# Eight PSUM banks divided anew, and row gathers asked for in fives, in a two-layer relational graph network on one core

## The chip, the cores and the metric

The kernel runs on one core of a Trainium2 chip. A core has a matrix engine (TensorE, PE in the profile, with its weight loads as PEld), VectorE (DVE), ScalarE (ACT), GpSimd (POOL) and SyncE (SP), which issues transfers. They run side by side, each in its own order, and wait for one another through semaphores. TensorE writes its results into PSUM, which has eight banks of 128 partitions by 512 numbers of 32 bits. VectorE and ScalarE read them from there.

The metric is the time of one execution on the device, in microseconds (us). Lower is better.

## The reference

50,000 nodes with 128 features each and 850,000 edges with a relation out of 16. The edges are sorted by destination, and each node has an edge to itself. Two layers of a relational graph convolution are followed by a residual sum and a layer norm:

```
def _rgcn_layer(h, src, dst, rel, basis, w_comp, loop_w, bias):
    W = jnp.einsum('rb,bio->rio', w_comp, basis)
    seg = dst.astype(jnp.int32) * N_REL + rel.astype(jnp.int32)
    agg = jax.ops.segment_sum(h[src], seg, num_segments=N_ENT * N_REL)
    agg = agg.reshape(N_ENT, N_REL, -1)
    msg = jnp.einsum('nri,rio->no', agg, W)
    out = msg + h @ loop_w + bias
    return jax.nn.relu(out)

h = _rgcn_layer(x, src, dst, rel, basis1, w_comp1, loop_w1, bias1)
h = _rgcn_layer(h, src, dst, rel, basis2, w_comp2, loop_w2, bias2)
x = _layernorm(x + h, axis=-1)
```

There are 8 bases. In words: for each edge the row of its source node is fetched, weighted by 8 numbers that belong to its relation, summed by destination, multiplied by the 8 bases and added up.

## The kernel before

**Tiles and chunks.** The edges other than those of a node to itself stand in tiles of 128. Ten tiles are a chunk (`K = 10`), and a layer has 625 chunks (`C`), 6,250 tiles in all. Since the edges are sorted by destination, a tile touches few nodes. It has 12 slots (`WN`), and a chunk has 120 (`S`).

**Gathers.** For each tile GpSimd issues one indirect transfer (`gather`, line 178) that fetches 128 rows of 128 numbers from `x` in layer one and from `H1` in layer two (`g<-in_x_dram,src` and `g<-H,src` in the profile). The rows land in one of 30 tiles `g0` to `g29` (`RING * PER`, 6 by 5). A tile `g` is free again when the product with it has run. At the start of a layer 30 gathers are issued at once (line 956). After that, `fetch` (lines 939 to 943) is called at line 996 after each chunk's last product, for the ten tiles that lie three chunks ahead. Of the ten gathers the first waits for TensorE, and this one wait covers all ten. `row_of` (line 934) says which of the 30 tiles a gather takes: on every second turn through the ring the order within ten is reversed, so that the first gather of a ten takes the tile whose product ran last.

**Products.** For each tile TensorE multiplies the 128 rows with `hot` (line 982), 128 by 96: for each edge its slot and its 8 weights. A product takes two passes, which the profile counts as two matmuls. Five products fill a bank `pa` of the pool `ps_a`, and ScalarE copies it into `aT` (line 999). `hot` is made by VectorE at line 872 two chunks ahead, from the weights of lines 596 and 625 (`weights`, every second chunk).

**Work beside the products.** TensorE's order is written out by hand: `ordered` at line 859 keeps the order in which the program names the instructions. After each of a chunk's ten products `beside` (line 911) takes one step of generators. With t as the tile's place in the chunk, these are:

- `owning` at t = 4 and 9: steps of `from_itself` (line 661), which handles groups of 512 nodes. Four transposes go into a bank `po` (line 676, two, a `yield`, two more). ScalarE copies them out (line 680). Eight matmuls follow with the bases (line 691), one for each step and each into a `po` of its own. VectorE reads each at line 698, and every second one is followed by the sum at line 706. There are 98 groups in a layer.
- `summing` at t = 1, 3, 6 and 9: steps of `slots_of_batch` (line 735), once for four chunks. The third step has the 8 matmuls of line 741 into a `po`, which ScalarE copies to `by_slot` (line 745). Six yields later four transposes go into one `po` (line 750, two in one step, two in the next), and VectorE reads it in two halves at line 724 (`spread_out`), a step apart. The last five chunks are handled one by one in `slots` (line 709).
- `weighing` at t = 5 and 8 of even chunks: lines 596 and 625.
- `ending` at t = 2, 6 and 9, and `add` at t = 8: `to_nodes` (line 774) adds slots to nodes in a bank `pn` (lines 785 and 795), and `finish` (line 802) writes a group's result.

In layer one, steps that read and sort the edges of chunks to come (`runs`, `rows_of`) are taken in between. They end in scatters by GpSimd (lines 355 and 410). At the end of layer one `count_up` (line 517) makes a checksum, with a matmul into a `po` at line 543.

**PSUM.** One bank holds weights and masks (`ps_c`), two are `ps_a`, three are `ps_o` (the tiles `po`) and two are `ps_n` (the tiles `pn`). A pool hands out its banks in turn. A matmul into a bank waits until the readers of the tile that had it before are done.

The other path, `summed`, runs only if the checksum fails. It does not run here.

Of the kernel before, what the change touches and what calls it, by code (L numbers as in the profile page):

```python
# [39 lines left out]
F32 = mybir.dt.float32  # L40
# [7 lines left out]
PSUM = bass.MemoryType.PSUM  # L48
DRAM = bass.MemoryType.DRAM

P = 128
# [3 lines left out]
K = P // WN  # L55
S = K * WN
# [8 lines left out]
PER = 5  # L65
# [18 lines left out]
def tile_rgcn_resnorm(  # L84
# [85 lines left out]

    LANDED = mybir.DependencyInfo(mybir.DependencyClass.Sync, mybir.DependencyReason.DATA)

    ps_a = ctx.enter_context(tc.tile_pool(name="ps_a", bufs=2, space=PSUM))
    ps_o = ctx.enter_context(tc.tile_pool(name="ps_o", bufs=3, space=PSUM))
    ps_n = ctx.enter_context(tc.tile_pool(name="ps_n", bufs=2, space=PSUM))

    def gather(to, of, idx):
# [391 lines left out]
    def chunked():  # L569
        with (  # L570
# [90 lines left out]
            def from_itself(g, of, n):  # L661

                m = nodes(g)
                h = sb.tile([P, J, D], F32, name="h_own", bufs=1)
                nc.sync.dma_start(h[:m], of_group(of, g))
                if g % T == 0:
                    for some in loop_weights(g, n):
                        if some is not None:
                            lws[:] = [some]
                        yield  # L670
                else:
                    yield
                lw = lws[0]
                po = ps_o.tile([P, BANK], F32, name="po")
                for j in range(J):
                    nc.tensor.transpose(po[:, j * P : j * P + m], h[:m, j, :], ident[:m, :m])
                    if j % 2:
                        yield
                hT = sb.tile([P, J, P], F32, name="hT", bufs=2)
                nc.scalar.copy(hT[:, :, :m], po.rearrange("p (j e) -> p j e", j=J)[:, :, :m])  # L680
                hTs[g] = hT
                yield
                ls = sb.tile([P, J, D], F32, name="ls")
                lss[g] = ls
                few = BANK // D
                if g == 0:
                    nc.vector.tensor_copy(by[:, NB, :], BIAS[n])
                for j in range(J):
                    for b in range(0, NB, few):
                        hb = ps_o.tile([P, BANK], F32, name="po")  # L690
                        nc.tensor.matmul(  # L691
                            hb[:m],
                            hT[:, j, :m],
                            BASIS[n][:, b : b + few, :].rearrange("p b d -> p (b d)"),
                            start=True,
                            stop=True,
                        )
                        nc.vector.tensor_tensor(  # L698
                            by[:m, b : b + few, :],
                            hb[:m].rearrange("p (b d) -> p b d", d=D),  # L700
                            lw[:m, j, g % T, b : b + few, None].to_broadcast([m, few, D]),
                            op=OP.mult,
                        )
                        if b + few < NB:
                            yield
                    nc.vector.tensor_reduce(ls[:m, j, :], by[:m].rearrange("p b d -> p d b"), AX.X, OP.add)  # L706
                    yield
# [27 lines left out]
            def slots_of_batch(c, aT, st, n):  # L735

                for _ in range(2):
                    yield
                ps = ps_o.tile([P, BANK], F32, name="po")
                for b in range(NB):  # L740
                    nc.tensor.matmul(  # L741
                        ps[:, : BATCH * S], BASIS[n][:, b, :], aT[:, b, :], start=b == 0, stop=b == NB - 1
                    )
                by_slot = sb.tile([P, BATCH * S], F32, name="by_slot", bufs=1)
                nc.scalar.copy(by_slot, ps[:, : BATCH * S])  # L745
                for _ in range(NB - 2):
                    yield
                po = ps_o.tile([P, BANK], F32, name="po")
                for q in range(BATCH):
                    nc.tensor.transpose(po[:S, q * P : (q + 1) * P], by_slot[:, q * S : (q + 1) * S], ident)  # L750
                    if q == 1:
                        yield
                for q in range(0, BATCH, 2):
                    pair = spread_out(c + q, pair_of_slots(), po[:, q * P : (q + 2) * P].rearrange("s (q d) -> s q d", q=2))
                    st[c + q], st[c + q + 1] = pair[:, 0], pair[:, 1]
                    yield

# [102 lines left out]
            for n, of in enumerate((x, H1)):  # L860
# [73 lines left out]
                def row_of(t):  # L934

                    turn, k = divmod(n * tiles + t, RING * PER)
                    return rows[k if turn % 2 == 0 else k // K * K + K - 1 - k % K]

                def fetch(some):

# [7 lines left out]
                for c in range(C):  # L948
# [27 lines left out]
                    for k in range(0, K, PER):  # L976
                        m = min(PER, ks(c) - k)
                        if m > 0:
                            pa = ps_a.tile([P, BANK], F32, name="pa")
                        for i in range(PER):  # L980
                            if i < m:
                                product = nc.tensor.matmul(  # L982
                                    pa[:, i * NB * WN : (i + 1) * NB * WN],
                                    row_of(c * K + k + i),
                                    hot[:, k + i].rearrange("e b w -> e (b w)"),
                                    start=True,
                                    stop=True,
                                )
                                if i == m - 2:
                                    tc.add_manual_dep(  # L990
                                        product.ins, fetched[c * K + k + m - 1].name, LANDED, reason="five at once"
                                    )
                            if i == m - 1:
                                if k + PER == K or m < PER:
                                    at = c * K + RING * PER
                                    fetch(range(at, at + K))
                                if n == 0 and c == 0 and k + PER == K:
                                    done(first_runs)
                                nc.scalar.copy(  # L999
                                    aT[:, :, place_of + k * WN : place_of + (k + m) * WN].rearrange(  # L1000
                                        "d b (i w) -> d i b w", w=WN
                                    ),
                                    pa[:, : m * NB * WN].rearrange("d (i b w) -> d i b w", i=m, w=WN),
                                )
                            beside(k + i, c, owning, summing, weighing)
# [208 lines left out]
```

## Time and profile before

| | |
|---|---|
| median of three runs | 15731.45 us |
| lowest, highest | 15729.49, 15732.01 us |
| the profiled execution | 15729.77 us |
| its span in the profile | 15728.0 us |
| granted TensorE clock | 0.815 |
| moved by transfers | 1004.74 MB, 64 GB/s |

The busiest groups, as sums over the span:

| line | engine | what | count | busy, us |
|---|---|---|---|---|
| 178 | POOL | gathers, both layers | 12,500 | 11826.3 |
| 982 | PE | products | 25,000 | 4896.0 |
| 785 | PE | slots to nodes | 4,128 | 3178.7 |
| 741 | PE | slots times bases | 4,960 | 2175.9 |
| 691 | PE | own rows times bases | 3,136 | 2002.8 |
| 625, 596 | DVE | weights | 1,252 | 3523.4 |
| 999 | ACT | copies of products | 2,500 | 1393.4 |

A row of a group reads: line, engine, operation, output `<-` inputs, sizes, `x` and the count, then busy us and the mean ns of one, then the idle time of the engine just ahead of these instructions and what ended most of it. In a row of the timeline the first number is the start in us from the begin of the span and the second the time, and the bracket holds the idle time ahead with its releaser. "issue" stands for time in which the engine waited for nothing that the profile shows.

### The profile page before, as it was taken

How to read it: one execution, taken by the hardware profiler on the slowest of the kernel's cores; microseconds unless marked ns; L12 is line 12 of the kernel's file. 1: busy time of each engine (PE TensorE's matmuls, PEld its weight loads, DVE VectorE, ACT ScalarE, POOL GpSimd, SP SyncE). 2: the span in 40 equal slices, each digit the busy share in tenths (PEclk: the TensorE clock that was granted, in tenths of full speed). 3: DMA queues.
4: the chain of work that ended last, by engine and by line, in shares of the span. 5: the costliest groups of instructions: out<-in, count | busy, mean ns of one | idle time of the engine just before them, and what ended most of it. 6: DMA issues, size and time to landing. Idle time of an engine off the chain costs nothing. (4 is left out here: it accounts for less than half of the span.)

```text
span 15728.0 us, 118277 instructions
## 1 busy us (share of the span) xinstructions
PE 11577.5 (74%) x41202; PEld 7072.9 (45%) x41202; DVE 10159.7 (65%) x10480; ACT 1937.9 (12%) x3683; POOL 11850.9 (75%) x12532
## 2 busy tenths in 40 slices
PE   5777777777777777777777777777777777777777
PEld 3444444444444444444444444444444444444444
DVE  7777776777655666566656666666666666666666
ACT  1111111111111111111111111111111111111111
POOL 7777777777777777777777777777777777777777
PEclk8888888888888888888878887888888888788888
DMA  2222222222222222222222222222222222222222
GB/s 83 71 71 66 72 66 71 67 67 70 62 60 60 60 60 60 60 60 60 59 58 63 64 63 62 63 63 63 63 63 63 62 62 63 63 63 63 62 63 61
DMA packets 539203, 1004.74 MB, mean 64 GB/s; under 512 B 261489, under 2 KB 264561, under 8 KB 538612
## 3 DMA queue, kind: packets, MB, share of 16 engines
q0 software_dynamic: 401872, 826.89, 18.4%
q1 hardware_dynamic: 133652, 168.42, 3.4%
q8 instruction: 343, 5.62, 0.1%
q14 instruction: 248, 2.03, 0.0%
q10 hardware_dynamic: 3088, 1.79, 0.0%
HBM read 924.65 MB, written 71.59 MB: 63 GB/s over the span
## 5 line engine op out<-in xcount | busy, mean ns | idle before, releaser
L982 PE MATMUL pa<-hot,g 128*128 128x96 f32 x25000 | 4896.0, 315 | 3996.9 <-DMA g<-H,src 1944.6
L178 POOL DMA_INDIRECT g<-in_x_dram,src x6250 | 5923.9, 948 | 1917.2 <-issue 1795.6
L178 POOL DMA_INDIRECT g<-H,src x6250 | 5902.4, 944 | 1917.6 <-issue 1807.9
L982 PEld LDWEIGHTS pa<-hot,g 128*128 128x128 f32 x25000 | 4312.8, 223 | 6609.3 <-issue 4156.2
L698 DVE TENSOR_TENSOR by<-po,lw 128x512 f32<-128x512 f32 x1568 | 1073.1, 685 | 3914.4 <-PE po L691 3913.5
L785 PE MATMUL pn<-slots,own 120*128 120x512 f32 x4128 | 3178.7, 905 | 84.9 <-DVE own L764 48.6
L999 ACT COPY aT<-pa 128x480 f32<-128x480 f32 x2500 | 1393.4, 557 | 10573.3 <-PE pa L982 10571.4
L741 PE MATMUL po<-aT,basis 128*128 128x480 f32 x4960 | 2175.9, 594 | 0.0
L691 PE MATMUL po<-basis,hT 128*128 128x512 f32 x3136 | 2002.8, 726 | 4.1 <-DVE by L698 3.2
L625 DVE TENSOR_REDUCE fixed<-terms 128x160 f32<-128x2560 f32 x626 | 1763.9, 2818 | 10.3
L596 DVE TENSOR_TENSOR terms<-kinds,fixed 128x2560 f32<-128x2560 uint8 x626 | 1759.5, 2811 | 11.1
L706 DVE TENSOR_REDUCE ls<-by 128x128 f32<-128x1152 f32 (+1 forms) x784 | 1659.8, 2117 | 33.2 <-DVE by L698 0.4
L872 DVE TENSOR_TENSOR hot<-fixed,own 128x960 f32<-128x960 f32 x1250 | 1437.1, 1150 | 34.2 <-PE pa L982 17.1
L741 PEld LDWEIGHTS po<-aT,basis 128*128 128x128 f32 x4960 | 973.4, 202 | 992.4 <-issue 992.4
L785 PEld LDWEIGHTS pn<-slots,own 120*128 120x128 f32 x4128 | 1019.9, 278 | 785.7 <-issue 687.3
L724 DVE TENSOR_TENSOR slots<-po,which 120x1024 f32<-120x1024 f32 (+1 forms) x630 | 761.2, 1208 | 544.9 <-PE po L750 524.8
L691 PEld LDWEIGHTS po<-basis,hT 128*128 128x128 f32 x3136 | 582.8, 232 | 9.5 <-ACT hT L680 5.3
L745 ACT COPY by_slot<-po 128x480 f32<-128x480 f32 x310 | 173.0, 558 | 2560.6 <-PE po L741 2551.6
L764 DVE TENSOR_SCALAR own<-col,node 120x256 f32<-120x256 f32 (+1 forms) x1250 | 435.7, 349 | 11.8 <-PE pn L785 11.8
L807 DVE TENSOR_TENSOR pn<-pn,ls 128x512 f32<-128x512 f32 x98 | 68.0, 693 | 487.3 <-PE pn L785 487.3
L795 PEld LDWEIGHTS pn<-loop,hT 128*128 128x128 f32 x1568 | 293.4, 261 | 169.1 <-issue 169.1
L807 DVE TENSOR_TENSOR ls<-pn,ls 128x512 f32<-128x512 f32 x98 | 67.1, 685 | 396.5 <-PE pn L785 396.5
(137 smaller groups left out, 3169.1 us busy)
## 6 DMA issues: line engine op xcount, KB each, us to landing
g<-in_x_dram,src POOLq DMA_INDIRECT x6250, 2.5
g<-H,src POOLq DMA_INDIRECT x6250, 2.5
h_own<-in_x_dram SPq DMA_DIRECT2D x97, 256.0 KB, 2.7
xw<-in_x_dram SPq DMA_DIRECT2D x97, 256.0 KB, 2.7
H<-ls SPq DMA_DIRECT2D x97, 256.0 KB, 2.1
h_own<-H SPq DMA_DIRECT2D x97, 256.0 KB, 2.7
out_dram<-ls SPq DMA_DIRECT2D x97, 256.0 KB, 2.5
FULL<-full SPq DMA_DIRECT2D x20, 640.0 KB, 4.5
```

Of the source, the lines that this page charges most:

```text
L178: return nc.gpsimd.indirect_dma_start(out=to, out_offset=None, in_=of, in_offset=bass.IndirectOffsetOnAxis(ap=idx, axis=0))
L596: nc.vector.tensor_tensor(terms, kinds[:, :, None, :].to_broadcast([P, k, NB, NR]), table[:, None, :, :].to_broadcast([P, k, NB, NR]), op= ...
L625: nc.vector.tensor_reduce(pm[:, :k], terms, AX.X, OP.add)
L691: nc.tensor.matmul(hb[:m], hT[:, j, :m], BASIS[n][:, b : b + few, :].rearrange("p b d -> p (b d)"), start=True, stop=True,)
L698: nc.vector.tensor_tensor(by[:m, b : b + few, :], hb[:m].rearrange("p (b d) -> p b d", d=D), lw[:m, j, g % T, b : b + few, None].to_broadc ...
L706: nc.vector.tensor_reduce(ls[:m, j, :], by[:m].rearrange("p b d -> p d b"), AX.X, OP.add)
L724: nc.vector.tensor_tensor(to[:k], of[:k, :, None, :].to_broadcast([k, pair, J, D]), which[:k, c : c + pair, :, None].to_broadcast([k, pair ...
L741: nc.tensor.matmul(ps[:, : BATCH * S], BASIS[n][:, b, :], aT[:, b, :], start=b == 0, stop=b == NB - 1)
L785: nc.tensor.matmul(sums[g], own, of[:k].rearrange("s j d -> s (j d)"), start=c == first(g), stop=c == final(g),)
L872: nc.vector.tensor_tensor(hot[:, : ks(c)], pm[:, : ks(c), :, None].to_broadcast([P, ks(c), NB, WN]), own[:, : ks(c), None, :].to_broadcast ...
L982: product = nc.tensor.matmul(pa[:, i * NB * WN : (i + 1) * NB * WN], row_of(c * K + k + i), hot[:, k + i].rearrange("e b w -> e (b w)"), s ...
L999: nc.scalar.copy(aT[:, :, place_of + k * WN : place_of + (k + m) * WN].rearrange("d b (i w) -> d i b w", w=WN), pa[:, : m * NB * WN].rearr ...
```

## The change

The pools `ps_a` and `ps_o` get four banks and one, in place of two and three. `from_itself` names its four transposes in one step. `slots_of_batch` takes a `po` for each pair of transposes and names its reader in the same step. `fetch` is called after each five products, for five tiles, the ones that take the tiles just used; and `row_of` reverses within fives. The rest of the first block of edges (`first_runs`) is named after the first five products of chunk 0, not after all ten.

```diff
@@ -170,8 +170,8 @@
-    ps_a = ctx.enter_context(tc.tile_pool(name="ps_a", bufs=2, space=PSUM))
-    ps_o = ctx.enter_context(tc.tile_pool(name="ps_o", bufs=3, space=PSUM))
+    ps_a = ctx.enter_context(tc.tile_pool(name="ps_a", bufs=4, space=PSUM))
+    ps_o = ctx.enter_context(tc.tile_pool(name="ps_o", bufs=1, space=PSUM))
     ps_n = ctx.enter_context(tc.tile_pool(name="ps_n", bufs=2, space=PSUM))
@@ -674,8 +674,6 @@
                 po = ps_o.tile([P, BANK], F32, name="po")
                 for j in range(J):
                     nc.tensor.transpose(po[:, j * P : j * P + m], h[:m, j, :], ident[:m, :m])
-                    if j % 2:
-                        yield
                 hT = sb.tile([P, J, P], F32, name="hT", bufs=2)
                 nc.scalar.copy(hT[:, :, :m], po.rearrange("p (j e) -> p j e", j=J)[:, :, :m])
@@ -745,13 +743,13 @@
                 nc.scalar.copy(by_slot, ps[:, : BATCH * S])
                 for _ in range(NB - 2):
                     yield
-                po = ps_o.tile([P, BANK], F32, name="po")
-                for q in range(BATCH):
-                    nc.tensor.transpose(po[:S, q * P : (q + 1) * P], by_slot[:, q * S : (q + 1) * S], ident)
-                    if q == 1:
-                        yield
                 for q in range(0, BATCH, 2):
-                    pair = spread_out(c + q, pair_of_slots(), po[:, q * P : (q + 2) * P].rearrange("s (q d) -> s q d", q=2))
+                    po = ps_o.tile([P, BANK], F32, name="po")
+                    for i in range(2):
+                        nc.tensor.transpose(
+                            po[:S, i * P : (i + 1) * P], by_slot[:, (q + i) * S : (q + i + 1) * S], ident
+                        )
+                    pair = spread_out(c + q, pair_of_slots(), po[:, : 2 * P].rearrange("s (q d) -> s q d", q=2))
                     st[c + q], st[c + q + 1] = pair[:, 0], pair[:, 1]
                     yield
@@ -934,7 +932,7 @@
                     turn, k = divmod(n * tiles + t, RING * PER)
-                    return rows[k if turn % 2 == 0 else k // K * K + K - 1 - k % K]
+                    return rows[k if turn % 2 == 0 else k // PER * PER + PER - 1 - k % PER]
@@ -991,10 +989,9 @@
                             if i == m - 1:
-                                if k + PER == K or m < PER:
-                                    at = c * K + RING * PER
-                                    fetch(range(at, at + K))
-                                if n == 0 and c == 0 and k + PER == K:
+                                at = c * K + k + RING * PER
+                                fetch(range(at, at + PER))
+                                if n == 0 and c == 0 and k == 0:
                                     done(first_runs)
                                 nc.scalar.copy(
```

## The prediction

> **What bounds the kernel now.** The page comes first: the busy time of each engine, the forty slices and the chain that ended last.
>
> ```profile
> PE 11577.5 (74%) x41202; PEld 7072.9 (45%) x41202; DVE 10159.7 (65%) x10480; ACT 1937.9 (12%) x3683; POOL 11850.9 (75%) x12532
> ...
> DVE  7777776777655666566656666666666666666666
> ...
> POOL 31%; issue 12%; DMA 6%; PE 0%; DVE 0%; POOLq 0%; ACT 0%; DVEq 0%
> ```
>
> GpSimd (POOL) and TensorE (PE) are equally busy, so shares decide nothing. The chain, as far as it was followed, names GpSimd and "issue", time in which an engine waits for nothing that is seen. So I read GpSimd's instructions grouped by shape, then line 178, the gather, with first and last start.
>
> ```profile
> L178 POOL DMA_INDIRECT g<-in_x_dram,src x6250 | 5923.9, 948 | 1917.2 <-issue 1795.6 <-DMA g<-in_x_dram,src 100.6 <-PE pa L982 11.4
> L178 POOL DMA_INDIRECT g<-H,src x6250 | 5902.4, 944 | 1917.6 <-issue 1807.9 <-DMA g<-H,src 102.7 <-PE pa L982 6.7
> L410 POOL DMA_INDIRECT LREL<-l_rel,l_to x10 | 11.9, 1190 | 3.0 <-issue 2.7 <-DVE own L764 0.3
> L355 POOL DMA_INDIRECT FULL<-full,to_i x10 | 10.1, 1013 | 20.8 <-DVE full L353 18.1 <-issue 2.1 <-DVE l_word L399 0.3
> ```
> ```profile
> L178 POOL DMA_INDIRECT g<-in_x_dram,src x6250: 938/944/1746, 29.6 to 7888.6; - x196
> L178 POOL DMA_INDIRECT g<-H,src x6250: 940/944/1158, 7903.4 to 15709.3; - x196
> L178 POOLq EVENT_SEMAPHORE  x1253: 17/17/21357, 60.5 to 15690.8; - x179
> ```
>
> In the second layer 6,249 steps take 15709.3 - 7903.4 = 7805.9 us, 1.2491 us each: 0.944 busy and 0.30 of gap in front. They come at that distance without a break, so the kernel is a queue of 12,500 gathers. The span is 29.6 (before the first) + 7859.0 (layer one) + 14.8 (last gather of layer one to the first of layer two) + 7805.9 + 18.7 (after the last start) = 15728.0 us. Layer one has 7859.0 - 7805.9 = 53.1 us more. Of these, nine FULL scatters at 1.01 + 0.30 and ten LREL scatters at 1.19 + 0.30 take 26.7; of the other 26.4, gathers that ran longer make 5923.9 - 5902.4 = 21.5 and stalls about 5.
>
> Is GpSimd held by anyone? Two rows from the waits, GpSimd's and TensorE's:
>
> ```profile
> POOL g L178 <- PE pa L982: 18.1, 43, 4.7
> ```
> ```profile
> PE pa L982 <- DMA g<-H,src: 1944.6, 1771, 2.9
> PE pa L982 <- DMA g<-in_x_dram,src: 1889.6, 1713, 4.4
> PE pa L982 <- ACT aT L999: 49.3, 93, 0.8
> ```
>
> Columns: total us, times, longest. The products wait for rows to land 1,771 times in the 625 chunks of layer two: nearly three times a chunk TensorE has used up everything that was fetched. The other way round GpSimd is held 43 times in the whole run, 18.1 us, of which 43 x 0.30 is the gap that stands before every gather.
>
> **The change, part by part.** *Gathers in fives.* The count of gathers, rows and bytes stays. Gather 30 + 10q waited for product 10q + 9, 21 tiles back; gather 30 + 5q now waits for product 5q + 4, 26 tiles back. So TensorE may be 26 x 1.249 = 32.5 us late before a gather notices, not 26.2. What it can save is the stalls of that kind:
>
> ```profile
> 108.43 0.94 POOL L178 DMA_INDIRECT g<-in_x_dram,src  x1 [0.90 <-PE pa L982]
> ...
> 125.45 0.94 POOL L178 DMA_INDIRECT g<-in_x_dram,src  x1 [4.73 <-PE pa L982]
> ```
>
> Both are at the start: 0.60 + 4.43 = 5.0 us beyond the usual gap. The second is the gather of tile 70, which waited for product 49, behind the matmuls of line 741 (a batch's third step, at tile 6); product 44 stands ahead of them. I take -5.0 (0 if the stall comes back at the next five; at most -26.4, all that layer one loses). The next gathers behind it need product 49, done before they are due.
>
> The price is a wait on TensorE's semaphore for each five, some 1,250 more on GpSimd's queue. Their rows read 17 ns at the median. A gather that carried one:
>
> ```profile
> 15696.80 0.94 POOL L178 DMA_INDIRECT g<-H,src  x1 [0.30 <-issue]
> 15698.04 0.95 POOL L178 DMA_INDIRECT g<-H,src  x1 [0.30 <-PE pa L982]
> 15699.30 0.95 POOL L178 DMA_INDIRECT g<-H,src  x1 [0.30 <-issue]
> ```
>
> 1.24 us after its predecessor, like the one behind it: the wait is taken while the gather before runs. I take 0; if that cover is gone, 1,250 x 0.017 = 21 us. The reversal of rows in fives moves which tile is reused, and adds no instruction. The first LREL scatter goes out five gathers earlier (6.2 us), which lets the first groups start earlier and is on no path of the gathers.
>
> *Four banks for products.* They take away waits like the 49.3 us above on an engine that then waits for rows: 0.
>
> *One bank for all else.* This adds waits: a matmul into `po` must now wait until VectorE or ScalarE has read the last one. Behind the waiting matmul stand the products, behind them ScalarE's copies `aT` and, 26 tiles on, the gathers. The readers, from VectorE's groups and from the list of tile `po`:
>
> ```profile
> L625 DVE TENSOR_REDUCE fixed<-terms 128x160 f32<-128x2560 f32 x626 | 1763.9, 2818 | 10.3
> L596 DVE TENSOR_TENSOR terms<-kinds,fixed 128x2560 f32<-128x2560 uint8 x626 | 1759.5, 2811 | 11.1
> L706 DVE TENSOR_REDUCE ls<-by 128x128 f32<-128x1152 f32 (+1 forms) x784 | 1659.8, 2117 | 33.2 <-DVE by L698 0.4
> L872 DVE TENSOR_TENSOR hot<-fixed,own 128x960 f32<-128x960 f32 x1250 | 1437.1, 1150 | 34.2 <-PE pa L982 17.1 <-DVE fixed L625 0.5
> L698 DVE TENSOR_TENSOR by<-po,lw 128x512 f32<-128x512 f32 x1568 | 1073.1, 685 | 3914.4 <-PE po L691 3913.5
> L724 DVE TENSOR_TENSOR slots<-po,which 120x1024 f32<-120x1024 f32 (+1 forms) x630 | 761.2, 1208 | 544.9 <-PE po L750 524.8 <-PE po L713 20.0
> ```
> ```profile
> L745 ACT COPY by_slot<-po x310: 558/558/560, 124.6 to 15662.1; 128x480 f32<-128x480 f32 x155
> L680 ACT COPY hT<-po x196: 438/592/595, 108.7 to 15643.5; 128x512 f32<-128x512 f32 x194, 128x336 f32<-128x336 f32 x2
> ```
>
> 1568 + 630 + 310 + 196 = 2,704 uses of the bank, 2.16 a chunk. What slack has TensorE? Two stages, busy us of PE, PEld, DVE, ACT, POOL:
>
> ```profile
> 1000.00:2000.00 1000.00, 729.69 (x2610) 444.90 (x2609) 734.41 (x888) 119.42 (x214) 756.98 (x798) 0.82 0.24 71
> 11000.00:12000.00 1000.00, 738.02 (x2622) 448.33 (x2622) 624.09 (x629) 128.01 (x253) 756.18 (x801) 0.81 0.22 63
> ```
>
> Per ten gathers (12.49 us) it is idle 3.37 and 3.27 us. So the mean added wait per use must stay under 3.27 / 2.16 = 1.5 us. From below it is 0: the five products between most uses cover a read of 0.685. From above a use waits for the read and one long VectorE operation ahead of it, 0.69 + 2.82 = 3.5 us, which is 7.6 us a chunk and too much. Which? By the code a batch of four chunks uses the bank at tiles 4, 6, 9 / 4, 9 / 1, 3, 4, 9 / 4, 9. Where VectorE has most to do, between tiles 4 and 9 of an even chunk, it gets lines 596, 625, 698, 706 and then 872: 2.81 + 2.82 + 0.69 + 2.12 + 1.15 = 9.6 us, and the next use is ten gathers, 12.5 us, after tile 4: no wait. Where the uses are closest, from tile 9 of the second chunk on, it has 0.69 + 2.12 + 1.15 = 4.0 us and reads the first pair (line 724) until 5.2; tile 3 comes four gathers after tile 9, at 5.0, and waits 0.2. The second pair is read until 6.4, and tile 4 comes at 6.2: 0.2 again. That is under 0.5 us a batch; for what else stands in VectorE's queue (new edges, finished groups) I take 1.0 us a chunk. It lies under the idle time and nearer the lower end, delays products that have 32.5 us, and costs the end 0. The transposes in one go let ScalarE read at once, and end a group's steps earlier.
>
> The Trainium skill (Perfetto Trace Analysis, section Matmuls) speaks against this part: independent matmul groups should rotate through different banks so that evacuating one overlaps the matmuls of the next. With no such overlap left, the reads above add 1568 x 0.685 + 630 x 1.208 + 310 x 0.558 + 196 x 0.592 = 2,124 us to TensorE, 1.70 a chunk; the trace so far agrees that a full set of banks costs waits, and by the rule the sum is the same, because 1.70 is under 3.27.
>
> *Between the layers, and the end.* Here TensorE's order is on the path:
>
> ```profile
> 7888.63 0.94 POOL L178 DMA_INDIRECT g<-in_x_dram,src  x1 [0.30 <-issue]
> 7889.59 0.65 POOL L521 IOTA even<- 1x625 f32 x1
> 7903.40 0.95 POOL L178 DMA_INDIRECT g<-H,src  x1 [13.16 <-issue]
> ```
> ```profile
> 7893.18 1.02 PE L713 MATMUL po<-basis,aT 128*120 128x128 f32 x7
> ```
> ```profile
> 7893.36 0.14 DVE L546 TENSOR_SCALAR off<-po 1x1 f32<-1x1 f32 x1
> ```
>
> Line 713 now needs the bank of line 543's `total`, read until 7893.50: +0.4 us. In the last chunks the uses lie about a chunk's half apart and the last group's products end earlier; I take 0, with -3 to +6 from a wait of this kind that is seen with three banks:
>
> ```profile
> 15676.53 3.64 PE L713 MATMUL po<-basis,aT 128*120 128x128 f32 x16 [3.65 <-DVE by L698]
> ```
>
> *Sum:* -5.0 + 0 + 0 + 0.4 + 0 = -4.6 us. The profiled execution took 15729.77 (span 15728.0 and 1.77 around it): 15725.2. The median of the runs shown is 1.7 above it, so 15727 us.
>
> **The rivals.** *A, TensorE becomes the bound where VectorE is fullest: slower.* Place: the first ten of the forty slices, where VectorE's digits are 7 and 6: 3,932 us or, at 7859.0 / 625 = 12.6 us, 312 chunks. VectorE is busy 734 of 1,000 us there, not 624. It decides from a mean wait of 3.37 / 2.16 = 1.56 us per use. With half a long operation ahead of each read, 0.69 + 1.41 = 2.1 us, a chunk takes 9.11 + 4.54 = 13.65, 1.16 over, 362 us in all; halfway from the threshold, 180 us: 15,907. For it: VectorE is left 266 of 1,000 us there, 3.3 a chunk, with the steps on new edges queued ahead of its reads. Against it: the count for a batch, and TensorE's speed when it has a backlog, beside that after a wait, eight matmuls and four:
>
> ```profile
> 15701.53 3.63 PE L785 MATMUL pn<-slots,own 120*128 120x512 f32 x8
> ```
> ```profile
> 5018.78 3.67 PE L785 MATMUL pn<-slots,own 120*128 120x512 f32 x4
> ```
>
> Eight take what four took: lateness shrinks TensorE's work.
>
> *B, the added waits on GpSimd's queue are not hidden.* At 17 ns 15,748; at three times that, 64 us, 15,791. Against it the gather at 15698.04.
>
> *C, all of layer one's stalls go:* 15,705. Against it: 21.5 of the 26.4 are longer gathers, not waits.
>
> *D, a gather itself gets quicker,* by over 2.5 ns each, 31 us or more: 15,696. No row shows one of 12,500 that depends on how many were asked for at once (medians 944 and 944).
>
> **How the numbers follow.** Forecast 0.78, A 0.12, B 0.05, C 0.03, D 0.02. A measurement of this kernel tells about 0.2% from no change, 31 us. Forecast and C lie within it, and B with half its chance: same 0.83. Slower: A and some of B, 0.14. Faster: D and a rest, 0.03. The range goes from 15,712 (half of the stalls of layer one) to 15,765 (+21 for the waits, +6 at the end, +6 in layer one, and a few us of A), which leaves out most of A, some of B, and D.
>
> **What would show it.** In the profile after, right: the second layer's gathers still 1.249 us apart; no 4.73 us stall before tile 70; some 2,500 semaphore rows at line 178; TensorE waiting for VectorE before `po` matmuls for 500 to 2,100 us, and as much less for landed rows. Wrong, by A: rows "POOL g <- PE" of tens of us. Wrong, by B: gathers 1.25 us apart become 1.27 at each fifth. Wrong in the sum: a longer stretch from 7888.6 or after the last gather.

## The result, and the profile after

The changed kernel took 15765.31 us (median of 17 executions, 15759.65 to 15771.35), the kernel before beside it 15729.79 (17, 15727.42 to 15733.83). The ratio is 1.0022, 95% interval 1.0015 to 1.0029: slower by 35.5 us, where 4.6 us less were forecast, and 0.3 us above the upper end of the range. The profiled execution took 15767.24 us, with a span of 15765.4.

The same view as before, line 178 of the changed kernel by shape (min, median and max ns, then the first and the last start):

```profile
L178 POOL DMA_INDIRECT g<-in_x_dram,src x6250: 940/944/1787, 29.7 to 7894.4; - x196
L178 POOL DMA_INDIRECT g<-H,src x6250: 940/944/1083, 7921.4 to 15729.1; - x196
L178 POOLq EVENT_SEMAPHORE  x2500: 17/17/43, 61.1 to 15714.9; - x193
```

The kernel is still a queue of gathers of 0.944 us. Taken apart as in the prediction:

| stretch, us | before | after | difference |
|---|---|---|---|
| before the first gather | 29.6 | 29.7 | +0.1 |
| gathers of layer one, first to last start | 7859.0 | 7864.7 | +5.7 |
| last start of layer one to first of layer two | 14.8 | 27.0 | +12.2 |
| gathers of layer two | 7805.9 | 7807.7 | +1.8 |
| behind the last start | 18.7 | 36.3 | +17.6 |
| span | 15728.0 | 15765.4 | +37.4 |

Nearly all is lost where a layer ends. There GpSimd is also held, which its timeline shows (start, us, and in brackets the idle time ahead):

```profile
7876.90 0.94 POOL L178 DMA_INDIRECT g<-in_x_dram,src  x1 [2.86 <-PE pa L980]
...
7921.38 0.95 POOL L178 DMA_INDIRECT g<-H,src  x1 [25.39 <-issue]
...
15709.88 0.94 POOL L178 DMA_INDIRECT g<-H,src  x1 [3.24 <-PE pa L980]
...
15724.11 0.94 POOL L178 DMA_INDIRECT g<-H,src  x1 [2.06 <-PE pa L980]
```

Three gathers wait for products (line 980 is line 982 of before). Less the 0.30 us that stands ahead of any gather, they lose 2.6 us in layer one and 4.7 in layer two, and these sit in the rows +5.7 and +1.8. So TensorE is later than the 32.5 us that the fives allow. What TensorE waited for, over the whole run (us, times, longest):

```profile
PE pa L980 <- DMA g<-H,src: 1111.1, 1038, 2.8
PE pa L980 <- DMA g<-in_x_dram,src: 969.5, 891, 4.4
PE po L749 <- DVE slots L722: 845.3, 256, 7.2
PE pn L783 <- DVE own L762: 382.7, 226, 6.5
PE po L689 <- DVE by L696: 330.4, 176, 10.7
PE po L739 <- DVE by L696: 302.2, 140, 5.9
PE po L689 <- DVE slots L722: 219.9, 194, 2.1
PE po L749 <- DVE by L696: 56.9, 156, 0.4
```

The `po` rows together are 1,755 us, against 10.1 for VectorE's reads before:

```profile
PE po L713 <- DVE by L698: 6.6, 2, 3.7
...
PE po L691 <- DVE by L698: 3.2, 1, 3.2
...
PE po L691 <- DVE slots L724: 0.3, 2, 0.2
```

The waits for landed rows fell by as much, from 3,834 to 2,081. In the middle of a layer that is an even exchange of idle time. At the end it isn't. TensorE in the last chunks (start, us, matmuls):

```profile
15675.04 2.00 PE L689 MATMUL po<-basis,hT 128*84 128x512 f32 x2 [3.31 <-DVE by L696]
15676.83 1.01 PE L980 MATMUL pa<-hot,g 128*128 128x96 f32 x4
...
15684.32 1.09 PE L689 MATMUL po<-basis,hT 128*84 128x512 f32 x2 [0.58 <-DVE by L696]
15685.24 0.36 PE L980 MATMUL pa<-hot,g 128*128 128x96 f32 x2
15688.75 8.37 PE L739 MATMUL po<-aT,basis 128*128 128x480 f32 x16 [3.15 <-DVE by L696]
15696.96 0.36 PE L980 MATMUL pa<-hot,g 128*128 128x96 f32 x2
15697.82 1.09 PE L689 MATMUL po<-basis,hT 128*84 128x512 f32 x2 [0.51 <-ACT by_slot L743]
...
15702.95 0.43 PE L749 MATMUL po<-ident,by_slot 128*120 128x128 f32 x2 [2.82 <-DVE slots L722]
```

and VectorE in the same time:

```profile
15677.08 0.69 DVE L696 TENSOR_TENSOR by<-po,lw 84x512 f32<-84x512 f32 x1 [2.09 <-PE po L689]
...
15684.30 2.11 DVE L704 TENSOR_REDUCE ls<-by 84x128 f32<-84x1152 f32 x1
15686.33 1.14 DVE L870 TENSOR_TENSOR hot<-fixed,own 128x960 f32<-128x960 f32 x1
15687.39 0.62 DVE L762 TENSOR_SCALAR own<-col,node 120x256 f32<-120x256 f32 x2
15687.93 0.67 DVE L696 TENSOR_TENSOR by<-po,lw 84x512 f32<-84x512 f32 x1
15698.95 0.69 DVE L696 TENSOR_TENSOR by<-po,lw 84x512 f32<-84x512 f32 x1 [10.35 <-PE po L689]
```

The two engines take turns. The matmul of 15684.32 (`hb`, a group's own rows times the bases) fills the bank. VectorE has a reduction, `hot` and `own` ahead of the read, which comes at 15687.93. Only then can line 739 begin, at 15688.75. ScalarE empties the bank, the next `hb` follows at 15697.82, and VectorE, which has that `hb` next in its order, has stood still for 10.35 us. The 79 steps from product 12,420 to the last one took 110.9 us; the same 79 took 94.9 before (all engines' busy us in that stretch, PE, PEld, DVE, ACT, POOL; first before, then after):

```profile
15617.30:15712.20 94.90, 77.87 (x338) 51.94 (x337) 65.98 (x81) 12.60 (x26) 70.37 (x75) 0.87 0.21 61
```
```profile
15638.60:15749.50 110.90, 82.36 (x333) 52.50 (x332) 62.83 (x77) 12.52 (x26) 65.74 (x70) 0.82 0.17 49
```

The lateness of each product can be worked out from the trace: the start of the i-th product less the start of the i-th gather. Means over the ten tiles of a chunk, layer two, us:

```
chunk             616   617   618   619   620   621   622   623   624
before            5.0   4.7   4.2   4.5   9.9  11.7  11.8   9.1   5.6
after             6.8  14.3  15.3  20.4  31.4  31.5  35.1  30.1  24.2
```

It rises at chunk 617, in layer one as in layer two. 617 is `ALONE - 3`, from where `beside` gives `owning` four steps a chunk (t = 0, 2, 4 and 9) and not two. A second step up lies at 620 (`ALONE`), from where the slots of two chunks are added to the nodes in each chunk; the kernel before has one there too (4.5 to 9.9), about half as high.

### The profile page after: what moved, and what is told of

The parts are those of the page before. It is cut to its first block, busy times and chain, and to the rows that moved or that the text cites. A ratio compares the mean times of both kernels' runs of the same rounds, so it can differ in the third digit from the quotient of the medians.

```text
span 15765.4 us, 118606 instructions
## 1 busy us (share of the span) xinstructions
PE 11368.1 (72%) x41202; PEld 7017.4 (45%) x41202; DVE 10211.6 (65%) x10480; ACT 1938.4 (12%) x3683; POOL 11856.1 (75%) x12532
## 5 line engine op out<-in xcount | busy, mean ns | idle before, releaser
L980 PEld LDWEIGHTS pa<-hot,g 128*128 128x128 f32 x25000 | 4176.8, 224 | 4397.9 <-issue 3192.1
L980 PE MATMUL pa<-hot,g 128*128 128x96 f32 x25000 | 4472.4, 310 | 2172.3 <-DMA g<-H,src 1111.1
L783 PE MATMUL pn<-slots,own 120*128 120x512 f32 x4128 | 2904.7, 834 | 389.8 <-DVE own L762 382.7
L739 PE MATMUL po<-aT,basis 128*128 128x480 f32 x4960 | 2333.1, 629 | 302.8 <-DVE by L696 302.2
L689 PE MATMUL po<-basis,hT 128*128 128x512 f32 x3136 | 2074.7, 749 | 560.3 <-DVE by L696 330.4
L704 DVE TENSOR_REDUCE ls<-by 128x128 f32<-128x1152 f32 (+1 forms) x784 | 1659.2, 2116 | 36.3
L739 PEld LDWEIGHTS po<-aT,basis 128*128 128x128 f32 x4960 | 1025.8, 213 | 1411.1 <-issue 1299.0
L783 PEld LDWEIGHTS pn<-slots,own 120*128 120x128 f32 x4128 | 951.5, 260 | 1072.9 <-issue 638.9
L749 PE MATMUL po<-ident,by_slot 128*120 128x128 f32 x1240 | 316.9, 345 | 911.2 <-DVE slots L722 845.3
L749 PEld LDWEIGHTS po<-ident,by_slot 128*120 128x120 f32 x1240 | 145.6, 161 | 995.5 <-DVE slots L722 889.9
```

The costliest lines, as they stand in the source:

```text
L689: nc.tensor.matmul(hb[:m], hT[:, j, :m], BASIS[n][:, b : b + few, :].rearrange("p b d -> p (b d)"), start=True, stop=True,)
L739: nc.tensor.matmul(ps[:, : BATCH * S], BASIS[n][:, b, :], aT[:, b, :], start=b == 0, stop=b == NB - 1)
L783: nc.tensor.matmul(sums[g], own, of[:k].rearrange("s j d -> s (j d)"), start=c == first(g), stop=c == final(g),)
L980: product = nc.tensor.matmul(pa[:, i * NB * WN : (i + 1) * NB * WN], row_of(c * K + k + i), hot[:, k + i].rearrange("e b w -> e (b w)"), s ...
```

## The experiments

Theory T (ends): the loss comes from the single bank in the last eight chunks of each layer. Rivals: R1, the depth of the fives lets TensorE be later; R2, the lateness is built up over the whole layer; R3, the transposes in one go move the last groups' steps; R4, the waits on GpSimd's queue cost time.

### First session: a chip on which the kernel before took 18,007 us

Four kernels. The first is the kernel before with only this:

```diff
-                    return rows[k if turn % 2 == 0 else k // K * K + K - 1 - k % K]
+                    return rows[k if turn % 2 == 0 else k // PER * PER + PER - 1 - k % PER]
...
-                                if k + PER == K or m < PER:
-                                    at = c * K + RING * PER
-                                    fetch(range(at, at + K))
-                                if n == 0 and c == 0 and k + PER == K:
+                                at = c * K + k + RING * PER
+                                fetch(range(at, at + PER))
+                                if n == 0 and c == 0 and k == 0:
```

> Edit: the kernel before (two banks for products, three for the rest, transposes as they were) with the gathers and the turning of the rows in fives. Stretches of the profile after, against before: layer one's gathers 7864.7 against 7859.0 us, from its last gather to the first of layer two 27.0 against 14.8, layer two 7807.7 against 7805.9, behind its last gather 36.3 against 18.7. Theory T (ends): the whole loss comes from the single bank: in the last eight chunks of each layer, where the last two groups' steps go at four a chunk and not two, TensorE and VectorE take turns at it, and TensorE falls 25 to 38 us behind the gathers. Then this kernel loses nothing: 14.8 +-1 and 18.7 +-2 at the two ends, the stall of 4.73 us before the gather of tile 70 away, 15,722 to 15,731 us. Rival R1 (depth): the fives let TensorE be 26 tiles late, not 21, and that is what comes due at the ends: 15,745 to 15,765, with 25 us and more at each end. Rival R4 (semaphores): 1,250 more waits on GpSimd's queue show as a longer step: layer two over 7,810.

The second is the changed kernel with these lines turned back.

> Edit: the changed kernel (four banks for products, one for the rest, transposes in one go) with the gathers and the turning of the rows in tens again. T (ends): the loss stays: 15,760 to 15,775 us; GpSimd is held earlier, because ten gathers wait for a product 21 tiles back and TensorE is up to 38 us late, so some of the loss moves from behind the last gather into the gathers, and the stall near tile 70 is there again (+5). R1 (depth): the loss goes, 15,725 to 15,740. R2 (steady): if the lateness of the steady stretch matters (up to 24 us in the first quarter with one bank, where tens allow 26), GpSimd is held there too, tens of us in all: 15,780 to 15,830.

The third is the changed kernel with

```diff
-    ps_a = ctx.enter_context(tc.tile_pool(name="ps_a", bufs=4, space=PSUM))
-    ps_o = ctx.enter_context(tc.tile_pool(name="ps_o", bufs=1, space=PSUM))
+    ps_a = ctx.enter_context(tc.tile_pool(name="ps_a", bufs=3, space=PSUM))
+    ps_o = ctx.enter_context(tc.tile_pool(name="ps_o", bufs=2, space=PSUM))
```

> Edit: the changed kernel with three banks for products and two for the rest. T (ends): with a second bank a matmul into one runs while the other is read, so the turns are broken: 15,726 to 15,740 us, TensorE's waits for VectorE's reads under 300 us in all (2,150 with one bank), the ends within 4 us of before. R3 (order): the transposes in one go make a group's steps ten and not twelve, so that the last groups' products fall elsewhere among the last chunks; if that is the cause, the second bank leaves the loss: 15,755 to 15,768.

The fourth gives it a second bank for the chunk loop's `po` near the ends only:

```diff
-    ps_a = ctx.enter_context(tc.tile_pool(name="ps_a", bufs=4, space=PSUM))
+    ps_a = ctx.enter_context(tc.tile_pool(name="ps_a", bufs=3, space=PSUM))
+    ps_e = ctx.enter_context(tc.tile_pool(name="ps_e", bufs=1, space=PSUM))
...
+            def bank():
+                turn[0] += 1
+                return (ps_e if now[0] >= C - LAG - 3 and turn[0] % 2 else ps_o).tile([P, BANK], F32, name="po")
...
-                po = ps_o.tile([P, BANK], F32, name="po")
+                po = bank()
```

> Edit: the changed kernel with three banks for products, one for the rest, and a second one for the rest that is used in turn with it only from the ninth chunk before a layer's end. T (ends): what is lost is lost in those chunks, so the time comes back: 15,728 to 15,742 us, with TensorE's waits for VectorE still about 1,900 us and the median lateness of a product still 5 to 6 us before the end. R2 (steady): if the lateness was built up by the waits of the whole layer, a second bank for the last nine chunks of 625 changes little: 15,755 to 15,768.

None of the numbers was met. The kernel before took 18006.97 us here (9 executions), 14% more than elsewhere; in fives 17945.49 (ratio 0.9964, 0.9951 to 0.9978), banks only 18417.39 (1.0235, 1.0220 to 1.0251), two banks 17934.14 (0.9958, 0.9945 to 0.9972), second bank at the ends 18157.14 (1.0083, 1.0069 to 1.0097). Rows of the first of these kernels, from GpSimd's waits and from TensorE's ("remote": released by something that the trace doesn't hold):

```profile
POOL g L178 <- remote: 1820.7, 571, 6.1
POOL g L178 <- PE pa L982: 254.4, 112, 7.9
```
```profile
PE pa L982 <- ACT aT L998: 2169.3, 374, 24.4
...
PE pa L982 <- DMA g<-H,src: 20.7, 21, 1.9
```

TensorE hardly waits for rows, 20.7 us in layer two where it was 1,944.6, and GpSimd stands still before its gathers for some 2,000 us, most of them until a release that the trace doesn't hold; by the code a gather waits for a product. So TensorE is late here all the way (a product starts 28 us after its gather at the median, not 4), and it, not GpSimd, seems to set the pace. The ends can't be told from the rest, and T is not tested. What the session does show is the price of the two halves of the change where TensorE is late throughout. Fives for tens alone bring 61 us. One bank against two, outside the last nine chunks, costs 18157 - 17934 = 223 us. Why TensorE is late on this chip stays open; it is taken up in the last section.

### Second session: a chip with the times of the prediction

Three of the kernels again, and the last of them also the other way round. On this chip the kernel before took 15731.62 us (30 executions).

> The kernel before with gathers and the turning of the rows in fives and nothing else, once more, to be read where the kernel before takes some 15,730 us (in the first session it took 18,007, with TensorE 28 us late all the way, and the ends could not be told apart from the rest). Theory T (ends): the whole loss comes from the single bank in the last eight chunks of each layer; this kernel has 14.8 +-1 us between the layers' gathers, 18.7 +-2 behind the last one, no stall of 4.73 us before the gather of tile 70: 15,722 to 15,731 us. R1 (depth): TensorE may be 26 tiles late and not 21, which comes due at the ends: 15,745 to 15,765. R4 (semaphores): layer two's gathers take over 7,810 us, not 7,806.

15730.11 us, ratio 0.9998 (0.9989 to 1.0007): as T expects. Its gathers, and what GpSimd waited for:

```profile
L178 POOL DMA_INDIRECT g<-in_x_dram,src x6250: 940/944/1743, 29.8 to 7893.9; - x196
L178 POOL DMA_INDIRECT g<-H,src x6250: 940/944/1192, 7907.2 to 15712.7; - x196
```
```profile
POOL g L178 <- PE pa L982: 105.1, 345, 0.3
```

No gather waits longer than the usual 0.3, so the stall of 4.73 us is gone. Between the layers lie 13.3 us (a little under the 14.8 +-1 of T), behind the last start 18.7. R1 falls. Layer two takes 15712.7 - 7907.2 = 7805.5 us with some 625 more semaphores: R4 falls as well.

> The changed kernel with gathers and rows in tens again (four banks, one bank and transposes in one go stay). T (ends): 15,760 to 15,775 us; both ends late by 10 us and more each, part of it before the last gathers. R1 (depth): the loss goes with the fives: 15,725 to 15,740. R2 (steady): the lateness of the first quarter (up to 24 us with one bank, where tens allow 26) now stops gathers there: 15,780 to 15,830. In the first session this kernel was the slowest, 2.4% over the kernel before, which R2 would have to show here as stalls before gathers.

15773.49 us, 1.0026 (1.0015 to 1.0037). The loss stays with tens: 41.9 us over the kernel before, where the changed kernel lost 35.5. The longest two stalls of layer two:

```profile
15716.84 0.95 POOL L178 DMA_INDIRECT g<-H,src  x1 [9.59 <-PE pa L980]
...
15731.05 0.94 POOL L178 DMA_INDIRECT g<-H,src  x1 [2.01 <-PE pa L980]
```

The wait for a product 21 tiles back is reached earlier, so GpSimd loses 11.0 us before its last gathers and only 30.1 lie behind them. Layer one has a stall of 10.6 us before its last twenty gathers, and 19.4 us lie between the layers. R2's stalls over the first quarter aren't there: between the 160th gather and that one no gather waits over 2 us. Only in the first 131 gathers three stand still (by 7 us in all), which the fives spare.

> The changed kernel with three banks for products, one for the rest, and a second one for the rest used in turn with it only from the ninth chunk before a layer's end. T (ends): 15,728 to 15,742 us, the two ends within 4 us of the kernel before, while TensorE's waits for VectorE in the middle stay near 1,900 us and the median lateness at 5 to 6 us. R2 (steady): 15,755 to 15,768.

> The other way round: two banks for the rest in turn up to the ninth chunk before a layer's end, one bank from there on. T (ends): the loss is there although the middle waits little (TensorE for VectorE under 500 us in all): 15,755 to 15,768 us, 24 to 28 us between the layers' gathers and 33 to 38 behind the last one. R2 (steady): 15,728 to 15,742.

The fifth differs from the fourth in one sign:

```diff
-                return (ps_e if now[0] >= C - LAG - 3 and turn[0] % 2 else ps_o).tile([P, BANK], F32, name="po")
+                return (ps_e if now[0] < C - LAG - 3 and turn[0] % 2 else ps_o).tile([P, BANK], F32, name="po")
```

One bank except at the ends: 15729.71 us, 0.9999 (0.9990 to 1.0008). One bank only at the ends: 15759.90 us, 1.0019 (1.0009 to 1.0028). Gathers and two of TensorE's waits, first of the former, then of the latter (its lines are numbered seven on, gathers one on):

```profile
L179 POOL DMA_INDIRECT g<-in_x_dram,src x6250: 940/944/1747, 29.6 to 7893.8; - x196
L179 POOL DMA_INDIRECT g<-H,src x6250: 940/944/1072, 7907.2 to 15712.0; - x196
```
```profile
PE po L756 <- DVE slots L729: 832.8, 268, 7.2
...
PE po L696 <- DVE by L703: 306.8, 160, 10.7
```
```profile
L179 POOL DMA_INDIRECT g<-in_x_dram,src x6250: 940/944/1787, 29.9 to 7885.5; - x196
L179 POOL DMA_INDIRECT g<-H,src x6250: 940/944/1068, 7912.7 to 15723.5; - x196
```
```profile
PE po L696 <- DVE slots L729: 537.7, 165, 7.4
...
PE po L696 <- DVE by L703: 17.2, 11, 3.3
```

The first kernel has nearly all the waits of the changed one (1,695 us in its five `po` rows for VectorE, against 1,755) and none of the loss: 13.4 us between the layers, and its span of 15730.8 ends 18.8 behind the last start. The second has a third of the waits (580 us in the same five rows, over the 500 expected) and 28.3 us of the loss of 35.5, with all of what the two ends cost: 27.3 and 36.3. R2 falls, and R3 too, since the transposes in one go are in both. In the first, the last 79 steps take 95.0 us, as before:

```profile
15619.90:15714.90 95.00, 74.28 (x333) 49.27 (x332) 64.31 (x82) 12.49 (x26) 70.52 (x75) 0.87 0.23 60
```

### Third session: what takes turns with what

The kernel before took 15733.80 us (27 executions). First the last groups' steps, spread:

```diff
-                    if t in (4, 9) or c >= ALONE - 3 and t in (0, 2):
+                    if t in (4, 9) or c >= ALONE - 3 and t in (1, 6):
```

> The changed kernel with the last groups' extra steps at tiles 1 and 6 of a chunk in place of 0 and 2, so that with tiles 4 and 9 the four steps lie two or three products apart and not two, two, five and one. If the loss at the ends is a matter of bunching (two uses so close that the read between them has no cover): 15,735 to 15,750 us. If it is one of throughput (four steps of a group a chunk, each a matmul that waits for VectorE and a multiplication that waits for TensorE, cost more than the 12.5 us of ten gathers however they lie): 15,757 to 15,770 us, the last products still 30 us and more late.

15757.98 us, 1.0017 (1.0007 to 1.0026): throughput, at the lower edge of what was expected. 36.2 us still lie behind the last gather and 24.7 between the layers; the lateness of chunk 622 is 32.2 and not 35.1, and of the stalls ahead of the last gathers 1.7 us are left. 24.2 us are lost and not 35.5, so the bunching costs about a third, not most of the loss. No run kept the last groups at two steps a chunk, so that the four steps do the rest is read from the code and from where the lateness begins.

Then a bank for the groups' products alone:

```diff
-    ps_a = ctx.enter_context(tc.tile_pool(name="ps_a", bufs=4, space=PSUM))
+    ps_a = ctx.enter_context(tc.tile_pool(name="ps_a", bufs=3, space=PSUM))
+    ps_e = ctx.enter_context(tc.tile_pool(name="ps_e", bufs=1, space=PSUM))
...
-                        hb = ps_o.tile([P, BANK], F32, name="po")
+                        hb = ps_e.tile([P, BANK], F32, name="po")
```

> The changed kernel with three banks for products, one bank for the groups' products hb alone (line 689), and one for all other uses, all through. If the turns are those of hb with itself (each waits until VectorE, behind its reduction of 2.1 us, has multiplied the last one), most of the loss stays: 15,748 to 15,765 us. If they are between hb and a batch's steps (lines 711, 739, 749 and the transposes), which stand in VectorE's queue in another order than in TensorE's, the loss goes: 15,727 to 15,742 us, and the waits of line 749 for the slots' read (845 us) stay, since both its halves still share one bank.

15741.78 us, 1.0006 (0.9997 to 1.0015): just inside the second case, turns between `hb` and a batch's steps. 8.0 us over the kernel before are left of 35.5, which the interval doesn't tell from none; the profile shows 16.9 between the layers and 28.7 behind the last gather. TensorE's waits (lines one on):

```profile
PE po L750 <- DVE slots L723: 846.7, 270, 7.8
PE po L690 <- DVE by L697: 269.4, 147, 10.3
PE pn L784 <- DVE own L763: 104.0, 84, 6.1
```

Line 739's waits for `by` (302.2 us) are gone, and so are line 689's for the slots' read (219.9). So about three quarters of the loss come from `hb` and a batch's steps sharing one bank. The reason given for it ahead of the run, another order in VectorE's queue than in TensorE's, isn't what the trace shows: in the changed kernel all 2,198 reads of lines 696 and 722 stand in VectorE's order just as TensorE fills the bank, and so do ScalarE's 506. The rows of the last chunks, shown with the result, have another reason: the read comes late, behind a reduction, `hot` and `own`, and with one bank the next user has to wait for it, whoever it is. What is left is not `hb` alone. In the last 79 steps of this kernel TensorE waits 8.8 us for a read of `hb` before the next, and 7.9 us for the slots' read before the transposes.

Last, two banks throughout, as in the first session's third kernel:

> The changed kernel with three banks for products and two for all other uses, to be read where the kernel before takes some 15,730 us. T (ends): the turns are broken everywhere: 15,724 to 15,736 us, TensorE's waits for VectorE under 500 us in all, both ends within 3 us of the kernel before. R3 (order): if the transposes in one go, which stay, are the cause: 15,755 to 15,768.

15724.05 us (11 executions, 15721.68 to 15727.37); the 27 of the kernel before lie between 15729.13 and 15737.25. The ratio is 0.9994, interval 0.9985 to 1.0003: no execution overlaps, but the interval doesn't exclude no difference. It is the quickest kernel of the study, by some 10 us over the kernel before. Its gathers (the span is 15725.6):

```profile
L178 POOL DMA_INDIRECT g<-in_x_dram,src x6250: 940/944/1743, 30.2 to 7888.2; - x196
L178 POOL DMA_INDIRECT g<-H,src x6250: 940/944/1079, 7901.4 to 15705.2; - x196
```

13.2 us between the layers, 20.4 behind the last start. TensorE's `po` waits for VectorE are 551 us, 534 of them line 689's for the slots' read: over the 500 expected, and without effect. R3 falls again. Where the 10 us come from, its profile (of the slowest of the eleven executions) doesn't show.

The lateness by chunk, in all kernels that tell something of the ends (layer two, worked out as above):

```
chunk                        616   617   618   619   620   621   622   623   624
second bank at the ends      4.9   5.6   4.9   6.4  11.4   7.6  11.3   7.5   4.3
one bank at the ends         7.3  15.4  16.4  21.6  32.6  32.7  36.3  30.6  24.2
even spacing                 6.8  12.0  13.0  15.0  27.7  28.5  32.2  28.6  24.2
own bank for hb              5.0   8.5   8.7  13.5  20.4  19.3  23.0  19.4  15.8
```

## Why the prediction was wrong, by its own steps

The time lies only 0.3 us above the range, but that is no near miss of the mechanism. Most of the upper end was +21 for waits on GpSimd's queue, which didn't come; its +6 at the end is a fifth of the 29.8 us that came there.

**What bounds the kernel: right.** Between the ends both kernels are the same queue of gathers. The second layer's are still 1.249 us apart.

**Gathers in fives: right.** The first 80 steps from gather to gather took 108.9 us before, 104.3 after and 104.6 in fives alone: -4.6, where -5.0 was forecast. It doesn't show in the total. In the profiled executions without stalls near the end layer one's gathers lie between 7855.6 and 7864.2 us, because gathers that run longer differ from run to run (5923.9 us busy before, 5934.5 in fives alone). The semaphores cost nothing, as forecast. What the step didn't price is what the deeper fives are worth once TensorE is late: 6.4 us (41.9 lost with tens against 35.5, each over its own runs of the kernel before).

**Four banks for products: 0, right.** Three served as well.

**One bank for all else: covered as forecast, sized too low, and used where a mean doesn't hold.** The estimate was 1.0 us a chunk; the `po` rows give 1,755 / 1,250 = 1.40, still under the 3.27 of idle time. They are made up otherwise than told: 845 us are line 749's second pair, which waits 3.3 us at a time (845.3 / 256) for the read of the first, where 0.2 was put down. The middle of a layer bears it: the kernel with the second bank at the ends has nearly the same waits and loses nothing.

**Between the layers, and the end: the step that failed.** It said that in the last chunks the uses lie about half a chunk apart, and took +0.4 and 0, with -3 to +6. The 0.4 itself is there (TensorE's wait for line 546). The uses do not lie so. From chunk 617 on line 915 of before names `owning` at t = 0, 2, 4 and 9, in the very loop that the step was about, and the batch's steps go on beside it. So the pace of some two uses a chunk, right for the other 617 chunks, was carried over. The nearest row was at hand: with three banks line 713 waited 3.65 us for a read of `by`, and it was taken as the bound of the whole and not as the price of one use. Measured, TensorE is 17.5 us later at the last product: before, it started at 15712.2, 2.9 us after the last gather (15709.3); after, at 15749.5, 20.4 us after it (15729.1). With one bank in the last nine chunks alone it is 20.4 us as well (15743.97 and 15723.54). From the last product to the end it is 15.8 and 15.9 us: what follows is the same, so the lateness goes into the time undiminished. Between the layers the same: the last product of layer one starts at 7891.5 before and 7911.3 after, and the first gather of layer two follows 11.9 and 10.1 us later. +12.2 and +17.6 there, and 7.3 us of stalls ahead of the last gathers, are the 37. What else changed nearly cancels: -4.6 at the start, and gathers that ran 6.9 us longer in layer one and 2.8 shorter in layer two.

**The cover.** The step named the idle time of TensorE as the cover, 3.27 us a chunk, and 32.5 us of delay that no gather notices. Both are true of a chunk with chunks behind it. The last ones have none: delay that a gather doesn't notice is passed on to the end instead.

**The Trainium skill's rule** (Perfetto Trace Analysis, section Matmuls: independent matmul groups should rotate through different banks, so that the evacuation of one overlaps the matmuls of the next) was weighed against the mean, and so came to the same sum. At the ends the trace agrees with it: the last 79 steps took 110.9 us with one bank and 95.0 with two in turn. In the middle it agrees on the waits (1,695 us in the kernel with the second bank at the ends), which cost nothing.

**The rivals.** A, TensorE as the bound where VectorE is fullest: not so. The lateness there grew (median 7.1 us over gathers 500 to 3,200, 4.1 before; at most 24.1) and stayed within the fives' 32.5. Its mechanism is the right one, though, at another place: turns with VectorE, where the uses are densest and not where VectorE is busiest. B, C and D: the runs show none of them.

## What to carry to other kernels

A buffer that is taken away costs nothing as long as the engine that waits has idle time and the waits can be made up later. Check this where the work is densest and where nothing comes after it (the last chunks of each stage), not with the mean over the kernel, and read from the code which steps change their pace there. Two buffers used in turn were enough here, and on the chips where the kernel has slack one was too few only in the last eight or nine of 625 chunks: a shared buffer is dear where its reader comes late, behind other work in its queue, and nothing follows in which the engine that fills it could catch up.

## What the runs showed of the hardware that had not been expected

**One chip ran the kernel before in 18,007 us, others in 15,730.** In the fives alone the instructions of GpSimd and VectorE took as long as on the other chip (busy 11863.4 and 10172.0 us, there 11860.7 and 10158.7), at a granted clock of 0.762 beside 0.813. By an estimate from these, a clock lower by 6% makes TensorE's work in ten gathers 9.7 us and not 9.1, still under their 12.5. In the profiled execution of the fives alone TensorE stands still 763 times for 3 us or more, 5,225 us in all (the gaps between the end of one matmul and the start of the next in the trace); on the other chip the same kernel did so 26 times, for 148 us. Why stays open: what released GpSimd isn't in the trace ("remote"), and nothing was tried. What is shown is that a kernel with slack on one chip can be without it on another, and that the order of the variants changes: fives were worth 61 us there and 1.5 here, within the scatter.

**Matmuls run slower behind a wait of 3 us or more.** The sixteen of line 739 took 8.37 us at 15688.75, after a wait of 3.15. The same sixteen in the kernel before, with no wait ahead:

```profile
15655.37 6.63 PE L741 MATMUL po<-aT,basis 128*128 128x480 f32 x16
```

All 40 batches of line 739 that began behind a wait of 3 us or more took over 8 us, 9.06 at the median; the 108 behind a shorter one took 6.68 at the median, and the 162 without one 6.63. So a turn at the bank with so long a wait costs more than the wait. It isn't the only thing that slows them: in the kernel before none of the 310 batches waited, and 46 took over 8 us. Against that, the products and the sums to nodes, of which fewer now come behind a wait for rows, are busy for less time (4896.0 us before, 4472.4 after, and 3178.7, 2904.7), so that TensorE's busy time fell from 11577.5 us to 11368.1 although the kernel became slower.
